# A selective scan that writes its states over its inputs: one pool of eight tiles in place of three and four

## The chip, the cores and the metric

The kernel runs on one core of a Trainium2 chip. The metric is the device time of one execution in microseconds (us). Before the change it is 21,997.85 us, the median of three runs (21,988.34 to 22,036.88).

The engines are named as the profile names them: PE multiplies matrices, PEld loads its weights, DVE is the vector engine, ACT the scalar engine, POOL is GpSimd, and SP issues the transfers. [...] SBUF and PSUM are the on-chip memories; PE writes to PSUM.

## The reference

Eight images of 56 x 56 tokens with 192 channels go through two layers. The first is an attention with depthwise convolutions. The second is a selective scan in four directions (by rows, by columns, and both backwards), and nearly all of the time is spent there. Cut to what matters:

```python
# xs: the 384 inner channels of each token, in the order of the direction k
dts, Bs, Cs = jnp.split(x_dbl, [R, R + N], axis=2)          # N = 16 states
delta = jax.nn.softplus(dts @ dt_w + dt_bias)               # per channel and token
A = -jnp.exp(A_logs)                                        # per channel and state

def step(h, inp):                                           # one token after another
    u_l, d_l, B_l, C_l = inp
    dA  = jnp.exp(d_l[..., None] * A)
    dBu = d_l[..., None] * B_l[:, :, None, :] * u_l[..., None]
    h = dA * h + dBu
    y = jnp.sum(h * C_l[:, :, None, :], axis=-1)            # sum over the 16 states
    return h, y
# ... then the four directions are added, normalised, gated with silu(z) and projected
```

## The kernel before

An image is cut into seven chunks of T = 448 tokens, so that there are 8 x 4 x 7 = 224 steps (image b, direction k, chunk c). In each step 16 states n are worked through, one after another. The 384 channels are NJ = 3 blocks of 128 partitions; a tile of [128, 3, 448] float32 is one state.

The pools (a pool hands out its buffers in turn; a tile can be written again when all of its readers are done):

```python
s2 = ctx.enter_context(tc.tile_pool(name="s2", bufs=2))
s3 = ctx.enter_context(tc.tile_pool(name="s3", bufs=3))     # dbu, g
s4 = ctx.enter_context(tc.tile_pool(name="s4", bufs=4))     # bb, h
py = ctx.enter_context(tc.tile_pool(name="py", bufs=1, space=PSUM))   # y
pa = ctx.enter_context(tc.tile_pool(name="pa", bufs=2, space=PSUM))   # da
pb = ctx.enter_context(tc.tile_pool(name="pb", bufs=3, space=PSUM))   # "bank": ht, cm, all else
```

One step:

```python
for n in range(NST + 1):
    if n < NST:
        bb = s4.tile([128, T], F32, name="bb")                        # B of this state on all partitions
        nc.sync.dma_start(bb, rows[n, :].partition_broadcast(128))
        ...                                                           # cm: C of this state, for six states
        dbu = s3.tile([128, NJ, T], F32, name="dbu")
        nc.gpsimd.tensor_tensor(                                      # L652, POOL
            dbu, du, bb.unsqueeze(1).to_broadcast([128, NJ, T]), ALU.mult)
        h = s4.tile([128, NJ, T], F32, name="h")
        for j in range(NJ):
            da = pa.tile([128, 512], F32, name="da")
            nc.scalar.activation(da[:, :T], dl[:, j], AF.Exp,         # L657, ACT
                                 scale=acoef[:, k * NJ + j, n:n + 1])
            nc.vector.tensor_tensor_scan(                             # L659, DVE
                h[:, j, rev], da[:, 0:T][:, rev], dbu[:, j, rev],
                0.0 if ci == 0 else carry[:, j, n:n + 1], ALU.mult, ALU.add)
        nc.scalar.copy(newc[:, :, n:n + 1], h[:, :, last])            # L662, ACT: the state carried on
        done.append((n, h, cm))
    if n >= 1:
        add_state(*done[n - 1], y, ct)
    ...            # a part of prepare() for the next step, of finish() for the image before,
    ...            # and of front(), the first layer of the next image
```

How a state gets into y, summed by PE in PSUM. States 0, 6 and 11 are multiplied by C on DVE (L598), states 3, 8 and 13 on POOL (L601), the other ten are transposed by PE, scaled by ACT and transposed back:

```python
def add_state(n, h, cm, y, ct):
    if n in BY_DVE:
        nc.vector.tensor_tensor(h, h, cm[:, :T]..., ALU.mult)         # L598
    elif n in BY_POOL:
        for j in range(NJ):
            nc.gpsimd.tensor_tensor(h[:, j], h[:, j], cm, ALU.mult)   # L601
    if n in BY_DVE or n in BY_POOL:
        for j in range(NJ):
            nc.tensor.matmul(y[:, j, :T], ident, h[:, j], ...)        # L604
        return
    for s in range(SUB):                                              # four quarters of 112 tokens
        ht = bank("ht")
        for j in range(NJ):
            nc.tensor.transpose(ht[...], h[:, j, cols], ident)        # L611
        g = s3.tile([TP, DIN], F32, name="g")
        nc.scalar.activation(g, ht[:TP, :DIN], AF.Copy, scale=ct[:, s, n:n + 1])   # L613
        for j in range(NJ):
            nc.tensor.matmul(y[:, j, cols], g[...], ident[:TP, :TP], is_transpose=True, ...)  # L615
```

What the next step needs, made by prepare() during this one (px, then xd, then softplus as below, then du):

```python
dl = s2.tile([128, NJ, T], F32, name="dl")
e = s1.tile([128, NJ, T], F32, name="e")
ln = s1.tile([128, NJ, T], F32, name="ln")
for j in range(NJ):
    ...                                                               # pdt (PE, L573)
    nc.scalar.activation(e[:, j], pdt[:, :T], AF.Abs, bias=dtb[:, q])   # L575
    nc.scalar.activation(dl[:, j], pdt[:, :T], AF.Relu, bias=dtb[:, q]) # L576
nc.scalar.activation(e, e, AF.Exp, scale=-1.0)                        # L578
nc.scalar.activation(ln, e, AF.Identity, bias=one)                    # L579
nc.vector.scalar_tensor_tensor(e, ln, -1.0, e, ALU.add, ALU.subtract) # L580
nc.scalar.activation(ln, ln, AF.Ln)                                   # L581
nc.vector.tensor_tensor(dl, dl, e, ALU.subtract)                      # L582
nc.vector.tensor_tensor(dl, dl, ln, ALU.add)                          # L583
du = s2.tile([128, NJ, T], F32, name="du")
nc.gpsimd.tensor_tensor(du, dl, xs, ALU.mult)                         # L585, POOL
```

A step ends with an addition of y to yacc on DVE (L690 for k = 0, L693 for the others). In the steps with k = 0 the image before is finished: means by PE, `yc` on DVE (L479), its square `sq` on POOL (L481), the variance by PE (L494), `yc` scaled on DVE (L498, L500), times the gate on POOL (L501), then the projection `pout` on PE (L510, L513), copied to `ot` by ACT (L516). In the other steps of images 0 to 6, and in all steps of image 0, a slice of front() for the next image is worked in.

The program is written in the order above, but the instructions of each engine are put into its queue by a scheduler, which takes into account how many buffers there are.

Of the kernel before, what the change touches and what calls it, by code (L numbers as in the profile page):

```python
# [8 lines left out]
F32 = mybir.dt.float32  # L9
AF = mybir.ActivationFunctionType  # L10
ALU = mybir.AluOpType
# [10 lines left out]
T = 448  # L22
# [12 lines left out]
NJ = DIN // 128  # L35
# [12 lines left out]
def kernel(  # L48
# [24 lines left out]
    nc = tc.nc  # L73
# [7 lines left out]
    def fill(name, shape, value):  # L81
        t = const.tile(shape, F32, name=name)
        nc.vector.memset(t, value)
        return t
# [5 lines left out]
    one = fill("one", [128, 1], 1.0)  # L90
# [81 lines left out]
    s1 = ctx.enter_context(tc.tile_pool(name="s1", bufs=1))  # L172
    s2 = ctx.enter_context(tc.tile_pool(name="s2", bufs=2))
    s3 = ctx.enter_context(tc.tile_pool(name="s3", bufs=3))
    s4 = ctx.enter_context(tc.tile_pool(name="s4", bufs=4))
    py = ctx.enter_context(tc.tile_pool(name="py", bufs=1, space=PSUM))
    pa = ctx.enter_context(tc.tile_pool(name="pa", bufs=2, space=PSUM))
    pb = ctx.enter_context(tc.tile_pool(name="pb", bufs=3, space=PSUM))
# [2 lines left out]
    def bank(name):  # L181
        return pb.tile([128, 512], F32, name=name, tag="bank")
# [337 lines left out]
    def finish_pools(b):  # L520
        es = ExitStack()
        c1 = es.enter_context(tc.tile_pool(name=f"c1_{b}", bufs=1))
        c2 = es.enter_context(tc.tile_pool(name=f"c2_{b}", bufs=2))
        return es, (c1, c2, scaled_weights(c1, 1, made[b]["rstd"]))
# [9 lines left out]
    def view(t, k, c):  # L534

        if k % 2 == 0:
            return t[:, :, c * T:(c + 1) * T].rearrange("p j (a b) -> p j a b", b=HW)
        return t.rearrange("p j (h w) -> p j w h", w=HW)[:, :, c * RPC:(c + 1) * RPC, :]
# [3 lines left out]
    def prepare(b, k, c, i):  # L542

        xs = s2.tile([128, NJ, T], F32, name="xs")
        nc.sync.dma_start(xs, made[b]["xcs"][k % 2][:, :, c * T:(c + 1) * T])
        if i == 0:
            dtw = s2.tile([R, DIN], F32, name="dtw")
            nc.sync.dma_start(dtw, dt_wT[:, k, :])
            dtws[k] = dtw
        yield {}  # L550
        px = bank("px")
        for j in range(NJ):
            nc.tensor.matmul(px[:NR, :T], xpw[:, k, j], xs[:, j], start=(j == 0), stop=(j == NJ - 1))
        xd = s2.tile([NR, T], F32, name="xd")
        nc.scalar.copy(xd, px[:NR, :T])
        rows = dchunk.tile([2 * NST, T], F32, name="rows")
        nc.sync.dma_start(rows, xd[R:NR, :])
        st = {"xs": xs, "xd": xd, "rows": rows}
        yield st

        pct = bank("pct")
        for s in range(SUB):
            nc.tensor.transpose(pct[:TP, s * NR:(s + 1) * NR], xd[:, s * TP:(s + 1) * TP], ident[:NR, :NR])
        ct = s2.tile([TP, SUB, NST], F32, name="ct")
        nc.scalar.copy(ct, pct[:TP, :SUB * NR].rearrange("p (s r) -> p s r", r=NR)[:, :, R + NST:NR])
        st["ct"] = ct

        dl = s2.tile([128, NJ, T], F32, name="dl")
        e = s1.tile([128, NJ, T], F32, name="e")
        ln = s1.tile([128, NJ, T], F32, name="ln")  # L570
        for j in range(NJ):
            pdt = bank("pdt")
            nc.tensor.matmul(pdt[:, :T], dtws[k][:, j * 128:(j + 1) * 128], xd[0:R, :], start=True, stop=True)  # L573
            q = k * NJ + j
            nc.scalar.activation(e[:, j], pdt[:, :T], AF.Abs, bias=dtb[:, q])  # L575
            nc.scalar.activation(dl[:, j], pdt[:, :T], AF.Relu, bias=dtb[:, q])  # L576
            yield st
        nc.scalar.activation(e, e, AF.Exp, scale=-1.0)  # L578
        nc.scalar.activation(ln, e, AF.Identity, bias=one)  # L579
        nc.vector.scalar_tensor_tensor(e, ln, -1.0, e, ALU.add, ALU.subtract)  # L580
        nc.scalar.activation(ln, ln, AF.Ln)  # L581
        nc.vector.tensor_tensor(dl, dl, e, ALU.subtract)  # L582
        nc.vector.tensor_tensor(dl, dl, ln, ALU.add)  # L583
        du = s2.tile([128, NJ, T], F32, name="du")
        nc.gpsimd.tensor_tensor(du, dl, xs, ALU.mult)  # L585
        st["dl"], st["du"] = dl, du
        yield st
# [30 lines left out]

    total = sum(front(0))
    cur = run_all(prepare(*steps[0]))  # L620
    carry = None
    fill, spent, given = None, 0.0, 0
    es = None
    for i, (b, k, c, ci) in enumerate(steps):
        if k == 0 and ci == 0:
            if b > 0:
                es, pools = finish_pools(b - 1)
            first_slot = 0 if b == 0 else NCH * NST
            fill = front(b + 1) if b + 1 < nb else iter(())
            spent, slot = 0.0, 0  # L630
        ending = finish(b - 1, c, pools) if k == 0 and b > 0 else iter(())
        ahead = prepare(*steps[i + 1]) if i + 1 < len(steps) else iter(())
        nxt = None
        rev = slice(None, None, -1 if k >= 2 else 1)
        last = slice(0, 1) if k >= 2 else slice(T - 1, T)
        dl, du, xd, rows, ct, xs = (cur[v] for v in ("dl", "du", "xd", "rows", "ct", "xs"))
        y = py.tile([128, NJ, 512], F32, name="y")
        newc = s2.tile([128, NJ, NST], F32, name="newc")
        done = []
        for n in range(NST + 1):  # L640
            if n < NST:
                bb = s4.tile([128, T], F32, name="bb")
                nc.sync.dma_start(bb, rows[n, :].partition_broadcast(128))
                cm = None
                if n in BY_DVE:
                    cm = bank("cm")
                    nc.tensor.matmul(cm[:, :T], sel[:, BY_DVE.index(n), :], xd, start=True, stop=True)  # L647
                elif n in BY_POOL:
                    cm = s2.tile([128, T], F32, name="cb")
                    nc.sync.dma_start(cm, rows[NST + n, :].partition_broadcast(128))  # L650
                dbu = s3.tile([128, NJ, T], F32, name="dbu")
                nc.gpsimd.tensor_tensor(  # L652
                    dbu, du, bb.unsqueeze(1).to_broadcast([128, NJ, T]), ALU.mult)
                h = s4.tile([128, NJ, T], F32, name="h")
                for j in range(NJ):
                    da = pa.tile([128, 512], F32, name="da")
                    nc.scalar.activation(da[:, :T], dl[:, j], AF.Exp,  # L657
                                         scale=acoef[:, k * NJ + j, n:n + 1])
                    nc.vector.tensor_tensor_scan(  # L659
                        h[:, j, rev], da[:, 0:T][:, rev], dbu[:, j, rev],  # L660
                        0.0 if ci == 0 else carry[:, j, n:n + 1], ALU.mult, ALU.add)
                nc.scalar.copy(newc[:, :, n:n + 1], h[:, :, last])  # L662
                done.append((n, h, cm))
            if n >= 1:
                add_state(*done[n - 1], y, ct)
            if n >= 2 and n % 2 == 0:
                nxt = next(ahead, nxt)
            if n < NST:
                for _ in range(2):
                    next(ending, None)  # L670
                slot += 1
                want = total * (slot - first_slot) / (NTOK - NST - first_slot)
                while spent < want:
                    got = next(fill, None)
                    if got is None:
                        break
                    spent += got
        for _ in ending:
            pass
        if k == 0 and ci == NCH - 1 and b > 0:  # L680
            es.close()
        if k == NDIR - 1 and ci == NCH - 2:
            for _ in fill:
                pass
        for st in ahead:
            nxt = st
        yv = view(yacc, k, c)
        if k == 0:
            for j in range(NJ):
                nc.vector.scalar_tensor_tensor(yacc[:, j, c * T:(c + 1) * T], xs[:, j], dsum[:, j], y[:, j, :T],  # L690
                                               ALU.mult, ALU.add)
        else:
            nc.vector.tensor_tensor(yv, y[:, :, :T].rearrange("p j (a b) -> p j a b", b=HW), yv, ALU.add)  # L693
        carry, cur = newc, nxt
# [63 lines left out]
```

## Time and profile before

The profiled execution took 21,992 us. Its core had a mean granted TensorE clock of 0.92 of full speed. From the groups of instructions:

| engine, line | what | count | mean ns | busy us |
|---|---|---|---|---|
| POOL L652 | dbu = du * B | 3584 | 3040 | 10,845.1 |
| POOL L601 | h * C, three states of 16 | 2016 | 1272 | 2,508.1 |
| DVE L659 | scan, with a carried state | 9216 | 1134 | 10,006.9 |
| DVE L659 | scan, first chunk | 1536 | 1072 | 1,579.6 |
| ACT L657 | da = exp(dl * A) | 10752 | 638 | 6,795.8 |
| ACT L613 | g = ht * C | 8960 | 576 | 4,786.1 |
| PE L611 | transposes into ht | 26880 | 288 | 4,483.0 |
| PE L615 | transposes back into y | 26880 | 281 | 4,360.3 |
| PE L604 | h into y by the identity | 8064 | 611 | 3,805.4 |

A line of the wait list reads: engine, tile and line that waited <- engine, tile and line that it waited for: us in total, how often, the longest. A line of the timeline reads: start, us taken, engine, line, operation, out<-in, shapes, and how many in a row; in brackets the idle time before, and what ended it. A wait for several things is put down to the one that came last.

### The profile page before, as it was taken

To read this page: it belongs to the slowest core of one execution; us is meant where nothing else is said; L and a number is where in the kernel's file an instruction comes from. 1 tells how busy PE (TensorE), PEld (TensorE's weight loads), DVE (VectorE), ACT (ScalarE), POOL (GpSimd) and SP (SyncE) were. 2 spreads that over 40 slices of the span, in tenths; PEclk is the share of its full clock that TensorE was granted. 3 is DMA by queue.
4 is the path that set the end of the run, shared out by engine and by line. 5 is a ranking of instruction groups with operands and counts; after the bars stand their busy time and mean duration, and the time that the engine had idled before them with its cause. 6 is when DMAs were issued, how large, how long until landed. Compare 5 with 4: busy or idle time off the path is not lost. (4 is left out here: it accounts for less than half of the span.)

```text
span 21990.5 us, 246125 instructions
## 1 busy us (share of the span) xinstructions
PE 18854.4 (86%) x84640; PEld 11005.3 (50%) x84640; DVE 15390.6 (70%) x14585; ACT 14548.1 (66%) x28166; POOL 14468.7 (66%) x6131
## 2 busy tenths in 40 slices
PE   8889888899888998889888899888988889887776
PEld 4454555545455455554555545555455554554444
DVE  1477777766677666876677766777667776677775
ACT  2467667666675766757666676666767667677665
POOL 0467677666676667766677666776667666677775
PEclk9899999999999999999999999999999999998888
DMA  1222222222222222222223222222222222222221
GB/s 50 82 66 66 67 84 65 74 62 65 82 68 71 63 69 77 81 61 61 73 75 80 60 62 73 76 77 62 61 84 68 76 61 61 81 70 67 61 61 41
DMA packets 935285, 1508.59 MB, mean 69 GB/s; under 512 B 102480, under 2 KB 917904, under 8 KB 930960
## 3 DMA queue, kind: packets, MB, share of 16 engines
q1 hardware_dynamic: 934032, 1492.83, 24.3%
q8 instruction: 670, 10.98, 0.2%
q14 instruction: 583, 4.78, 0.1%
HBM read 1322.38 MB, written 170.08 MB: 68 GB/s over the span
## 5 line engine op out<-in xcount | busy, mean ns | idle before, releaser
L652 POOL TENSOR_TENSOR dbu<-du,bb 128x1344 f32<-128x1344 f32 x3584 | 10845.1, 3040 | 4585.7 <-DVE h L659 2376.8
L659 DVE TENSOR_TENSOR_SCAN h<-da,newc,dbu 128x448 f32<-128x448 f32 x9216 | 10006.9, 1134 | 4142.2 <-PE ht L611 1467.0
L657 ACT ACTIVATE da<-dl,acoef 128x448 f32<-128x448 f32 x10752 | 6795.8, 638 | 3454.9 <-DVE h L659 3423.1
L613 ACT ACTIVATE g<-ht,ct 112x384 f32<-112x384 f32 x8960 | 4786.1, 576 | 1364.1 <-PE ht L611 1331.2
L615 PE MATMUL y<-ident,g 112*128 112x112 f32 x26880 | 4360.3, 281 | 1316.2 <-ACT g L613 1276.1
L611 PE MATMUL ht<-ident,h 128*112 128x128 f32 x26880 | 4483.0, 288 | 671.5 <-DVE h L659 182.1
L615 PEld LDWEIGHTS y<-ident,g 112*128 112x128 f32 x26880 | 2994.2, 147 | 3629.3 <-ACT g L613 3017.1
L604 PE MATMUL y<-h,ident 128*128 128x448 f32 x8064 | 3805.4, 611 | 473.2 <-DVE h L598 207.5
L611 PEld LDWEIGHTS ht<-ident,h 128*112 128x112 f32 x26880 | 3213.5, 141 | 1978.7 <-issue 1012.7
L601 POOL TENSOR_TENSOR h<-h,cb 128x448 f32<-128x448 f32 x2016 | 2508.1, 1272 | 1374.7 <-ACT newc L662 1374.7
L604 PEld LDWEIGHTS y<-h,ident 128*128 128x128 f32 x8064 | 1588.3, 211 | 2092.7 <-issue 1472.4
L659 DVE TENSOR_TENSOR_SCAN h<-da,dbu 128x448 f32<-128x448 f32 x1536 | 1579.6, 1072 | 676.2 <-PE ht L611 209.2
L662 ACT COPY newc<-h 128x3 f32<-128x3 f32 x3584 | 702.9, 196 | 1267.6 <-DVE h L659 1260.8
L215 PE MATMUL pcv<-xa,dg 128*128 128x440 f32 (+2 forms) x3024 | 1303.0, 545 | 0.3 <-ACT g L613 0.3
L388 PE MATMUL ps<-qT,kT 64*112 64x448 f32 x2352 | 1160.3, 605 | 70.3 <-DMA qT<-qd 38.3
L598 DVE TENSOR_TENSOR h<-h,cm 128x1344 f32<-128x1344 f32 x672 | 1035.9, 1542 | 255.8 <-PE cm L647 244.2
L396 PE MATMUL po<-pT,vt 112*128 112x448 f32 x2352 | 1043.1, 550 | 0.0
L585 POOL TENSOR_TENSOR du<-dl,xs 128x1344 f32<-128x1344 f32 x224 | 679.8, 3035 | 540.6 <-DVE dl L583 526.2
L391 ACT ACTIVATE pT<-ps,nsh 112x448 f32<-112x448 f32 x1176 | 726.1, 630 | 290.9 <-PE ps L388 237.8
L215 PE MATMUL pq<-band,dgq 96*96 96x440 f32 (+3 forms) x2016 | 866.4, 546 | 0.0
L647 PE MATMUL cm<-xd,sel 44*128 44x448 f32 x1344 | 712.0, 611 | 6.5 <-ACT dl L576 6.5
L573 PE MATMUL pdt<-xd,dtw 12*128 12x448 f32 x1344 | 708.0, 607 | 0.0
(140 smaller groups left out, 12929.0 us busy)
## 6 DMA issues: line engine op xcount, KB each, us to landing
bb<-rows SPq DMA_DIRECT2D x3584, 224.0 KB
cb<-rows SPq DMA_DIRECT2D x672, 224.0 KB
xt<-x1d SPq DMA_DIRECT2D x224, 336.0 KB
xs<-xch SPq DMA_DIRECT2D x112, 672.0 KB
xs<-xcw SPq DMA_DIRECT2D x112, 672.0 KB
xch<-xv SPq DMA_DIRECT2D x24, 1568.0 KB
xcw<-xw SPq DMA_DIRECT2D x168, 224.0 KB
xin<-in_x_dram SPq DMA_DIRECT2D x56, 336.0 KB
```

The lines of the kernel that those rows point to most:

```text
L215: nc.tensor.matmul(out[:, o0:o1, a:b], lhs, img(lo, hi)[:, :, a + dx - 1:b + dx - 1], start=(t == TAPS[0]), stop=(t == TAPS[-1]))
L388: nc.tensor.matmul(ps[:TP, :T], kh[rows, kb * TP:(kb + 1) * TP], qh[rows, :], start=True, stop=True)
L396: nc.tensor.matmul(po[:, :T], vt[:, kb, g:g + 2, :].rearrange("p g d -> p (g d)"), pts[kb], start=(kb == 0), stop=(kb == NKB - 1))
L598: nc.vector.tensor_tensor(h, h, cm[:, :T].unsqueeze(1).to_broadcast([128, NJ, T]), ALU.mult)
L601: nc.gpsimd.tensor_tensor(h[:, j], h[:, j], cm, ALU.mult)
L604: nc.tensor.matmul(y[:, j, :T], ident, h[:, j], start=(n == 0), stop=(n == NST - 1))
L611: nc.tensor.transpose(ht[:TP, j * 128:(j + 1) * 128], h[:, j, cols], ident)
L613: nc.scalar.activation(g, ht[:TP, :DIN], AF.Copy, scale=ct[:, s, n:n + 1])
L615: nc.tensor.matmul(y[:, j, cols], g[:, j * 128:(j + 1) * 128], ident[:TP, :TP], is_transpose=True, start=False, stop=(n == NST - 1 and s = ...
L652: nc.gpsimd.tensor_tensor(dbu, du, bb.unsqueeze(1).to_broadcast([128, NJ, T]), ALU.mult)
L657: nc.scalar.activation(da[:, :T], dl[:, j], AF.Exp, scale=acoef[:, k * NJ + j, n:n + 1])
L659: nc.vector.tensor_tensor_scan(h[:, j, rev], da[:, 0:T][:, rev], dbu[:, j, rev], 0.0 if ci == 0 else carry[:, j, n:n + 1], ALU.mult, ALU.add)
```

## The change

The scan writes each state over the product that it reads. A state then needs one tile from its product to its last reader, where it needed one tile in s3 from the product to the scan, and one in s4 from the scan to its last reader. The seven tiles become one pool of eight. The room for the eighth comes from `ln`, whose values are now kept in `du` until du itself is written. The change is for a freer use of the same memory: which part of the chain runs ahead is no longer fixed at three and four.

```diff
@@ -173,6 +173,7 @@
     s4 = ctx.enter_context(tc.tile_pool(name="s4", bufs=4))
+    s8 = ctx.enter_context(tc.tile_pool(name="s8", bufs=8))
@@ -567,7 +568,7 @@
-        ln = s1.tile([128, NJ, T], F32, name="ln")
+        du = s2.tile([128, NJ, T], F32, name="du")
...
-        nc.scalar.activation(ln, e, AF.Identity, bias=one)
-        nc.vector.scalar_tensor_tensor(e, ln, -1.0, e, ALU.add, ALU.subtract)
-        nc.scalar.activation(ln, ln, AF.Ln)
+        nc.scalar.activation(du, e, AF.Identity, bias=one)
+        nc.vector.scalar_tensor_tensor(e, du, -1.0, e, ALU.add, ALU.subtract)
+        nc.scalar.activation(du, du, AF.Ln)
         nc.vector.tensor_tensor(dl, dl, e, ALU.subtract)
-        nc.vector.tensor_tensor(dl, dl, ln, ALU.add)
-        du = s2.tile([128, NJ, T], F32, name="du")
+        nc.vector.tensor_tensor(dl, dl, du, ALU.add)
         nc.gpsimd.tensor_tensor(du, dl, xs, ALU.mult)
@@ -648,16 +648,15 @@
-                dbu = s3.tile([128, NJ, T], F32, name="dbu")
+                h = s8.tile([128, NJ, T], F32, name="h")
                 nc.gpsimd.tensor_tensor(
-                    dbu, du, bb.unsqueeze(1).to_broadcast([128, NJ, T]), ALU.mult)
-                h = s4.tile([128, NJ, T], F32, name="h")
+                    h, du, bb.unsqueeze(1).to_broadcast([128, NJ, T]), ALU.mult)
                 for j in range(NJ):
...
                     nc.vector.tensor_tensor_scan(
-                        h[:, j, rev], da[:, 0:T][:, rev], dbu[:, j, rev],
+                        h[:, j, rev], da[:, 0:T][:, rev], h[:, j, rev],
                         0.0 if ci == 0 else carry[:, j, n:n + 1], ALU.mult, ALU.add)
```

## The prediction

> **What bounds the kernel now.** I read the head of the page first, then the wait list, then the timeline of one step (448 tokens, one direction, 16 states) in each kind of stage.
>
> ```profile
> span 21990.5 us, 246125 instructions
> ...
> PE 18854.4 (86%) x84640; PEld 11005.3 (50%) x84640; DVE 15390.6 (70%) x14585; ACT 14548.1 (66%) x28166; POOL 14468.7 (66%) x6131
> ```
>
> No engine is full. [...] the rest stand at about two thirds. The time is made of engines waiting for each other, so next come the waits:
>
> ```profile
> ACT da L657 <- DVE h L659: 3423.1, 4200, 7.1
> PEld y L615 <- ACT g L613: 3017.1, 4588, 7.3
> POOL dbu L652 <- DVE h L659: 2376.8, 1006, 13.3
> DVE h L659 <- PE ht L611: 1676.1, 750, 8.9
> ...
> POOL h L601 <- ACT newc L662: 1374.7, 196, 17.7
> ...
> DVE h L659 <- PE y L604: 833.0, 391, 8.4
> ```
>
> Two are waits for buffers. The scan on DVE waits for PE to be done with the state four back (1676.1 + 833.0 = 2509 us, 11% of the span), and POOL's product waits for the scan three back (2376.8 us, on an engine with time to spare). Now the stages. The period of a step is the distance of two additions to yacc in the timeline. A step that carries a slice of the next image's first layer (I call it a fill step):
>
> ```profile
> 4963.67 1.55 DVE L693 TENSOR_TENSOR yacc<-y,yacc 128x1344 f32<-128x1344 f32 x1
> ...
> 5031.08 6.11 POOL L601 TENSOR_TENSOR h<-h,cb 128x448 f32<-128x448 f32 x3 [10.62 <-ACT newc L662]
> 5037.15 3.03 POOL L585 TENSOR_TENSOR du<-dl,xs 128x1344 f32<-128x1344 f32 x1
> ...
> 5058.22 1.53 DVE L693 TENSOR_TENSOR yacc<-y,yacc 128x1344 f32<-128x1344 f32 x1
> ```
>
> Here 94.6 us. A step of the last image, with no fill (one call of these: a bare step):
>
> ```profile
> 21048.36 1.53 DVE L693 TENSOR_TENSOR yacc<-y,yacc 128x1344 f32<-128x1344 f32 x1
> ...
> 21107.88 3.04 POOL L652 TENSOR_TENSOR dbu<-du,bb 128x1344 f32<-128x1344 f32 x1 [2.17 <-issue]
> 21107.94 4.40 DVE L580 SCALAR_TENSOR_TENSOR e<-ln,e 128x1344 f32<-128x1344 f32 x1 [0.18 <-ACT ln L579]
> ...
> 21117.43 3.02 POOL L585 TENSOR_TENSOR du<-dl,xs 128x1344 f32<-128x1344 f32 x1 [6.51 <-DVE dl L583]
> ...
> 21133.70 1.53 DVE L693 TENSOR_TENSOR yacc<-y,yacc 128x1344 f32<-128x1344 f32 x1
> ```
>
> 85.3 us, and du starts when the softplus chain (L580, L582, L583) ends. A step that also finishes the image before (k = 0):
>
> ```profile
> 19783.65 2.42 POOL L481 TENSOR_TENSOR sq<-yc 128x1344 f32<-128x1344 f32 x1
> ...
> 19806.17 3.02 POOL L501 TENSOR_TENSOR yc<-yc,zs 128x1344 f32<-128x1344 f32 x1 [1.76 <-DVE yc L500]
> ...
> 19809.24 2.15 PE L510 MATMUL pout<-outpw,yc 128*112 128x192 f32 x6 [2.27 <-POOL yc L501]
> ```
>
> Its period is 85.2 us (first yacc addition at 19774.08, then 19859.33); PE waits for POOL's yc. From the yacc additions over the span: 28 fill steps of the first image at 91.8 us, 126 later ones at 99.5, 49 finishing ones at 85.7, 21 bare ones at 84.1. With 757 us of start and 189 of end that is 22,019, near enough to the span.
>
> [...] L580 takes 1.53 us as a rule and 4.40 where it began 0.06 us after a dbu of 3.04. [...] I expect the same duration in place.
>
> **The change part by part.** (1) No instruction is added or removed: 3584 products, 10752 scans, the same matmuls. Using du for ln costs nothing (two buffers, and the old du is dead). (2) DVE no longer waits for a free h: the product's tile is the scan's. The wait moves to POOL, which now needs the state eight back to be through PE. (3) The order of each queue moves, as the compiled programs show. I write the states 0 to 15 for POOL's products, C3, C8, C13 for its multiplications by C, and name a step's queue on POOL:
> - bare: before du C13 0-6 C3 7-11 C8 12-15; after du C13 0-9 C3 10-14 C8 15. ACT, DVE and PE keep their order.
> - finishing: before du 0-4 sq 5 6 C3 7 yc 8-11 C8 12-15 C13; after du 0-7 sq 8 9 C3 10-12 yc 13 C8 14 15 C13.
> - fill: before du 0-6 C3 7-11 C8 12-15 C13; after mostly du 0-6 C3 7-10 C8 11-13 C13 14 15. Softplus on DVE moves from between scans 13 and 15 to behind scan 15. On ACT, g of a state stood on average 2.5 states behind da (at most 3.7), now 4.1 (at most 7.7).
>
> Bare steps, from the start of du: C3 began at 34.6 us. Ten products in a row behind C13 end at 6.3 + 10 x 3.04 = 36.7, so C3 is 2.1 later. C8 began at 57.95; product 14 needs state 6 through PE, now at about 55.3, so C8 begins at 58.3, +0.35. The last product is then long done when L580 comes, and L580 falls from 4.40 to 1.53 us on the chain that sets du: -2.87. Sum -2.5 us x 21 = -53 us.
>
> Finishing steps: yc waited only for DVE and began at 41.4 us after du. In the new queue C3 ends at 39.3 and three products stand ahead of yc: 39.3 + 3 x 3.04 = 48.4, 7 later. PE's queue has pout ahead of the next cm and transposes, ACT's has ot ahead of g of state 5, and ACT is all but full from there to du; I let 1.5 to 2 us be recovered: +5.3 us x 49 = +260 us.
>
> Fill steps: the slot waits on DVE go (seven of them, 13.9 us, in the step shown). What comes: scan 14 waits for scan 13, C13 (3.3) and product 14 (3.0), some 6.7 us; at the end of a step DVE waits for g of states 9 and 10 on ACT (about 9), the softplus on two engines (about 5.5), du and product 0 (6.1): some 17 us beyond the 67 us that DVE is busy in such a step. So the scan chain alone takes 67 + 6.7 + 17 = 91 us. PE needs some 84 of the 99.5. Two chains of 91 and 84 us coupled through eight buffers, with g queued far behind da, I put at 97, an estimate with 4 us of doubt: -2.5 x 126 = -315 us. The first image's steps, with less PE work, I leave as they are.
>
> Sum: -53 + 260 - 315 = -108 us, 21,890. As I have counted every new wait but not what the looser coupling does for the others, I take 21,850.
>
> **The rivals.** (a) The buffers were the bound: all of the 2509 us come back, up to 19,500. Against it: in the fill steps PE is idle only a tenth of the time, and bare steps have hardly any slot wait. Half of it would be 20,700. (b) The new POOL wait closes a longer loop: PE frees a tile, POOL writes it (3.0), DVE scans it (3.4), and only then comes the g that PE waits for, since ACT takes it after da of seven states on. Some 9 us for one state where 99.5 / 16 = 6.2 are needed. Where the queue stands at its deepest lag in most steps, fill steps go to 102 and the time to 22,450. (c) POOL was never the limit and PE's queue is the same, so nothing moves: 21,990.
>
> **Range and chances.** The fill steps carry the doubt: 4 us either way is 500 us. The finishing steps add 150. Range 21,200 to 22,500. Faster than 21,558 needs fill steps of about 94 or less: 0.27. Slower than 22,438 needs them at 101 with the finishing loss: 0.19. The rest 0.54.
>
> **What would show it.** "DVE h <- PE" nearly gone from the wait list, and "POOL h <- PE" grown. L580 at 1.5 us and a bare step at 82.9. A finishing step at 90 to 91, with PE's pout waiting some 9 us for yc. In fill steps a gap on DVE of some 6 us ahead of scan 14 and one of 15 us or more ahead of scan 0. I am wrong if fill steps fall below 93 (coupling was the cost) or the scan's own duration moves.

## The result and the profile after

The changed kernel takes 23,683.09 us (median of four runs, 23,672.54 to 23,687.91), the kernel before 22,007.75 beside it: a ratio of 1.0759, 95% interval 1.0741 to 1.0778. The prediction was 21,850 us, range 21,200 to 22,500.

The head of the page of the changed kernel:

```profile
span 23685.2 us, 249153 instructions
...
PE 19449.3 (82%) x84640; PEld 11326.1 (48%) x84640; DVE 15504.3 (65%) x14585; ACT 14590.6 (62%) x28166; POOL 14256.4 (60%) x6131
```

The same work is done: DVE, ACT and POOL are busy for about as long as before, PE for 595 us more, in a span that is 1,695 us longer. The scan in place has its old duration, as the prediction expected, and so has the product (1,134 and 3,040 ns before; the mean in ns is the number after the busy time, in the groups of instructions):

```profile
L652 POOL TENSOR_TENSOR h<-du,bb 128x1344 f32<-128x1344 f32 x3584 | 10810.0, 3038 | 3369.3 <-PE ht L611 2086.4
L658 DVE TENSOR_TENSOR_SCAN h<-da,newc,h 128x448 f32<-128x448 f32 x9216 | 9963.2, 1133 | 4361.8 <-POOL h L652 2821.0
```

So the time went into waits. From the wait list of the changed kernel (us in total, times, longest):

```profile
...
ACT da L656 <- DVE h L658: 3670.2, 3702, 11.4
DVE h L658 <- POOL h L652: 3306.1, 806, 11.7
POOL du L585 <- DVE dl L584: 2930.0, 143, 26.5
POOL h L652 <- PE ht L611: 2086.4, 605, 11.9
...
POOL h L601 <- ACT newc L661: 1644.6, 369, 16.6
...
DVE h L598 <- PE cm L647: 1266.9, 200, 14.6
...
POOL h L652 <- PE y L604: 737.6, 234, 15.8
```

The 2,509 us in which the scan waited for PE are gone, as they had to be. In their place the scan waits 3,306 us for POOL's product, and the product waits 2,824 us for PE (2,086.4 + 737.6). In the kernel before, the scan's wait for the product was 452 us:

```profile
DVE h L659 <- POOL dbu L652: 452.2, 201, 4.5
```

Where the time was lost is read from the yacc additions. The period of a step is the time from the start of the addition before it to the start of its own, counted the same way for both kernels; the very first step has no addition before it.

| steps | before, us | after, us | number | together, us |
|---|---|---|---|---|
| first image | 90.7 | 95.4 | 27 | +126 |
| finishing | 85.8 | 92.4 | 49 | +319 |
| fill | 99.2 | 109.5 | 126 | +1,290 |
| bare | 84.1 | 81.7 | 21 | -50 |

The last column is worked out from periods that are not rounded. Its sum is +1,685, the time ahead of the first addition and behind the last adds 9, and the spans differ by 1,695. Three quarters of the loss lies in the fill steps. Here is how one of them looks inside, in the timeline of the changed kernel:

```profile
5346.83 0.82 PE L611 MATMUL ht<-ident,h 128*112 128x128 f32 x6
...
5350.28 3.03 POOL L652 TENSOR_TENSOR h<-du,bb 128x1344 f32<-128x1344 f32 x1 [2.98 <-PE ht L611]
...
5353.34 2.19 DVE L658 TENSOR_TENSOR_SCAN h<-da,newc,h 128x448 f32<-128x448 f32 x2 [2.65 <-POOL h L652]
5354.52 0.64 ACT L656 ACTIVATE da<-dl,acoef 128x448 f32<-128x448 f32 x1 [2.68 <-DVE h L658]
5355.10 0.56 ACT L613 ACTIVATE g<-ht,ct 112x384 f32<-112x384 f32 x1
...
5355.71 0.68 PE L615 MATMUL y<-ident,g 112*128 112x112 f32 x3 [1.76 <-ACT g L613]
...
5358.88 1.04 PE L611 MATMUL ht<-ident,h 128*112 128x128 f32 x6
...
5360.00 3.03 POOL L652 TENSOR_TENSOR h<-du,bb 128x1344 f32<-128x1344 f32 x1 [6.70 <-PE ht L611]
...
5363.07 1.15 DVE L658 TENSOR_TENSOR_SCAN h<-da,newc,h 128x448 f32<-128x448 f32 x1 [5.03 <-POOL h L652]
```

Read the brackets downwards. The product waits for PE to transpose an old state out of its tile; the scan waits for the product; the decay factor on ACT waits for the scan (it needs the PSUM tile that the scan has read); the weighted copy g of an old state, which stands behind that decay factor in ACT's queue, comes next; PE's transposition back waits for g, and only then does PE transpose what frees the next tile. From one product to the next it is 5360.00 - 5350.28 = 9.7 us, where the product itself takes 3.03. This is the longest distance in the step. Over all fill steps a wait for PE ended ahead of 633 of the 1,890 products that follow another in their step, and these start a median of 7.7 us behind the one before. All four engines take turns. And at the end of the same step, on DVE:

```profile
5382.03 0.60 DVE L411 BATCH_NORM_STATS2 st<-x 96x6 f32<-96x448 f32 x1
5393.17 1.55 DVE L598 TENSOR_TENSOR h<-h,cm 128x1344 f32<-128x1344 f32 x1 [10.55 <-PE cm L647]
5395.05 1.56 DVE L581 SCALAR_TENSOR_TENSOR e<-du,e 128x1344 f32<-128x1344 f32 x1 [0.32 <-ACT du L580]
...
5398.59 1.56 DVE L584 TENSOR_TENSOR dl<-dl,du 128x1344 f32<-128x1344 f32 x1 [0.39 <-ACT du L582]
5406.39 2.19 DVE L658 TENSOR_TENSOR_SCAN h<-da,newc,h 128x448 f32<-128x448 f32 x2 [6.24 <-POOL h L652]
```

For 24 us DVE scans nothing, and it is idle for 17.5 of them (the brackets). Two things could be behind this picture, and they call for different cures: a ring of tiles (a pool's buffers, used in turn) that is used up, or a preparation of the next step that comes too late.

### The profile page after: what moved, and what is told of

It is laid out like the page before. It is cut to its first block, busy times and chain, and to the rows that moved or that the text cites. A ratio compares the mean times of both kernels' runs of the same rounds, so it can differ in the third digit from the quotient of the medians.

```text
span 23685.2 us, 249153 instructions
## 1 busy us (share of the span) xinstructions
PE 19449.3 (82%) x84640; PEld 11326.1 (48%) x84640; DVE 15504.3 (65%) x14585; ACT 14590.6 (62%) x28166; POOL 14256.4 (60%) x6131
## 5 line engine op out<-in xcount | busy, mean ns | idle before, releaser
L652 POOL TENSOR_TENSOR h<-du,bb 128x1344 f32<-128x1344 f32 x3584 | 10810.0, 3038 | 3369.3 <-PE ht L611 2086.4
L658 DVE TENSOR_TENSOR_SCAN h<-da,newc,h 128x448 f32<-128x448 f32 x9216 | 9963.2, 1133 | 4361.8 <-POOL h L652 2821.0
L615 PE MATMUL y<-ident,g 112*128 112x112 f32 x26880 | 4477.2, 288 | 1983.1 <-ACT g L613 1951.3
L615 PEld LDWEIGHTS y<-ident,g 112*128 112x128 f32 x26880 | 3086.8, 151 | 4339.8 <-ACT g L613 3709.0
L604 PE MATMUL y<-h,ident 128*128 128x448 f32 x8064 | 3986.9, 634 | 519.9 <-POOL h L601 276.4
L601 POOL TENSOR_TENSOR h<-h,cb 128x448 f32<-128x448 f32 x2016 | 2336.4, 1186 | 1648.2 <-ACT newc L661 1644.6
L604 PEld LDWEIGHTS y<-h,ident 128*128 128x128 f32 x8064 | 1665.8, 222 | 2317.3 <-issue 1547.2
L658 DVE TENSOR_TENSOR_SCAN h<-da,h 128x448 f32<-128x448 f32 x1536 | 1596.6, 1083 | 739.3 <-POOL h L652 485.1
L574 PE MATMUL pdt<-xd,dtw 12*128 12x448 f32 x1344 | 773.2, 658 | 32.1 <-DVE hkv L304 32.0
L216 PEld LDWEIGHTS pcv<-xa,dg 128*128 128x128 f32 x3024 | 551.9, 204 | 353.2 <-issue 335.8
```

The lines of the kernel that those rows point to most:

```text
L216: nc.tensor.matmul(out[:, o0:o1, a:b], lhs, img(lo, hi)[:, :, a + dx - 1:b + dx - 1], start=(t == TAPS[0]), stop=(t == TAPS[-1]))
L604: nc.tensor.matmul(y[:, j, :T], ident, h[:, j], start=(n == 0), stop=(n == NST - 1))
L615: nc.tensor.matmul(y[:, j, cols], g[:, j * 128:(j + 1) * 128], ident[:TP, :TP], is_transpose=True, start=False, stop=(n == NST - 1 and s = ...
L652: nc.gpsimd.tensor_tensor(h, du, bb.unsqueeze(1).to_broadcast([128, NJ, T]), ALU.mult)
L658: nc.vector.tensor_tensor_scan(h[:, j, rev], da[:, 0:T][:, rev], h[:, j, rev], 0.0 if ci == 0 else carry[:, j, n:n + 1], ALU.mult, ALU.add)
```

## The experiments

I call the lead the number of states by which ACT's queue has the decay factors da ahead of the weighted copy g. It is read from the compiled queues. ACT works through its queue in that order, for its records in the traces give the same leads: at most 3.67 before and 7.67 after (four and eight tiles less a third of a state). It grew only in the steps with fill: in the finishing steps it is at most 3.33 before and 3.67 after, in the bare ones 2 in both. C3, C8 and C13 are POOL's multiplications, as in the prediction; VectorE and GpSimd in the expectations are DVE and POOL. All ratios are to the kernel before, run beside each on the same chip (21,990 to 22,008 us). The last four columns are periods of a step in us.

| run | us | ratio, 95% interval | first image | finishing | fill | bare |
|---|---|---|---|---|---|---|
| before | 22,007.75 | 1 | 90.7 | 85.8 | 99.2 | 84.1 |
| after | 23,683 | 1.0759 (1.0741 to 1.0778) | 95.4 | 92.4 | 109.5 | 81.7 |
| e1_three_five | 22,224 | 1.0111 (1.0073 to 1.0148) | 91.9 | 85.2 | 101.0 | 84.1 |
| e5_two_six | 22,698 | 1.0326 (1.0289 to 1.0364) | 91.8 | 95.4 | 100.2 | 87.8 |
| e2_pool_6 | 24,901 | 1.1329 (1.1287 to 1.1370) | 104.8 | 90.5 | 118.8 | 76.2 |
| e6_cap4 | 21,771 | 0.9905 (0.9868 to 0.9942) | 88.8 | 92.4 | 95.8 | 81.7 |
| e7_pin | 23,289 | 1.0592 (1.0571 to 1.0613) | 95.4 | 85.4 | 109.1 | 81.7 |
| e8_cap_pin | 21,446 | 0.9757 (0.9741 to 0.9774) | 89.0 | 85.8 | 95.6 | 81.7 |
| e9_cap_pool6 | 21,505 | 0.9781 (0.9762 to 0.9801) | 87.5 | 90.2 | 95.5 | 76.4 |
| e10_cap6 | 21,984 | 1.0001 (0.9992 to 1.0010) | 90.4 | 92.4 | 97.0 | 81.7 |
| e11_c_late | 23,213 | 1.0550 (1.0525 to 1.0575) | 93.2 | 89.7 | 107.5 | 80.2 |
| e12_cap_c_early | 23,159 | 1.0525 (1.0499 to 1.0551) | 94.0 | 103.9 | 99.8 | 88.9 |
| e13_best | 21,230 | 0.9647 (0.9629 to 0.9665) | 87.5 | 85.3 | 95.5 | 76.1 |
| e3_early | 24,742 | 1.1244 (1.1211 to 1.1276) | 103.9 | 94.6 | 115.2 | 81.2 |

### Is it the lead or the sharing? Eight tiles that are not shared

e1_three_five is the kernel before with ln in du and five tiles for h; e5_two_six has two tiles for dbu and six for h.

```diff
...
-                h = s4.tile([128, NJ, T], F32, name="h")
+                h = s4.tile([128, NJ, T], F32, name="h", bufs=5)     # e5: dbu bufs=2, h bufs=6
```

> Eight tiles as in the changed kernel, but not shared: three for the scan's inputs and five for its states, and the scan writes to a tile of its own. ACT's queue puts the decay factors at most 4.67 states ahead of the weighted copy g (3.67 in the kernel before, 7.67 in the changed one), 3.2 on average (2.5 and 4.1). Theory D (the loss comes from how far the scans are queued ahead of what TensorE has to do with the states, so that the next step's preparation comes late): in proportion to the average, (3.16 - 2.52) / (4.1 - 2.52) = 0.4 of the loss, near 22,690 us. Theory S (the loss comes from the sharing, since a product must wait until TensorE has read the state in its tile): nothing is shared here, so no loss and 21,950 to 22,050 us. Rival P (VectorE and GpSimd disturb each other on one tile): as S.

> Two tiles for inputs and six for states, not shared. The decay factors run up to 5.67 states ahead, 3.67 on average. Theory D: (3.67 - 2.52) / 1.58 = 0.73 of the loss, near 23,240 us, and the wait of GpSimd's delta product for VectorE grows from 526 us of the kernel before to over 1,500 us. Theory S: no loss through states; two input tiles can cost a little on GpSimd, 22,000 to 22,300 us, and the wait for the delta product stays near 526 us.

Measured: 22,224 and 22,698 us. Neither theory has the numbers. The lead rose to 5.67 in e5_two_six, and the fill steps went up by only 1.0 us (99.2 to 100.2): a long lead by itself costs little, so D falls as a theory of the fill steps. Most of e5's loss is in the finishing steps (49 x 9.6 = 470 us), which D and S don't speak of; I did not take that apart.

### Fewer shared tiles

e2_pool_6 is the changed kernel with `bufs=6` for s8.

> The changed kernel with six shared tiles in place of eight. The decay factors run up to 5.67 states ahead, 3.5 on average. Theory D: 0.64 of the loss, near 23,090 us, faster than the changed kernel though it has fewer tiles. Theory S: a product waits for TensorE two states earlier, so at least as slow as the changed kernel, 23,700 to 24,500 us.

Measured: 24,901 us, fill steps 118.8, the scans' wait for products 6,020 us. D is refuted again, and S was too mild. The same lead of 5.67 costs 1 us in a fill step with tiles that are not shared, and some 20 with six that are (C8 and C13 also stand early there, which is worth a few of them, as shown below, and there are six tiles in all in place of eight).

### The lead held short, tiles and sharing kept

e6_cap4 gives ACT an order, and no wait: the third da of a state stands behind the last g of the state four earlier.

```diff
...
+                    gate = last_g[-4 if n == 0 else -3] if j == NJ - 1 and len(last_g) > 3 else None
+                    with tc.issue_after(gate) if gate is not None else ExitStack():
-                    nc.scalar.activation(da[:, :T], dl[:, j], AF.Exp,
-                                         scale=acoef[:, k * NJ + j, n:n + 1])
+                        nc.scalar.activation(da[:, :T], dl[:, j], AF.Exp,
+                                             scale=acoef[:, k * NJ + j, n:n + 1])
```

`last_g` holds the last g of each state, or that of the state before where a state has none.

> The changed kernel, eight shared tiles, with an order and no wait added on ACT: the third decay factor of a state is queued behind the last weighted copy of the state four earlier, so that the lead is at most 3.67 states as in the kernel before (2.7 on average), while the tiles and their sharing stay. Theory D: the loss goes, 21,950 to 22,300 us, the delta product's wait for VectorE falls from 2,930 us to near 526 us, and a fill step is back near 99 us. Theory S, and rival P (both engines on one tile): the tiles are shared as before, so 23,500 to 23,800 us.

Measured: 21,771 us, 1,912 less than the changed kernel and 1% below the kernel before. Theory D had 21,950 at the least. From its wait list, whole span:

```profile
...
POOL h L601 <- ACT newc L666: 2777.3, 261, 21.1
...
POOL du L585 <- DVE dl L584: 778.0, 95, 18.3
POOL h L655 <- PE y L604: 774.4, 327, 15.7
POOL h L655 <- PE ht L611: 666.0, 379, 17.1
...
DVE h L663 <- POOL h L655: 441.6, 188, 4.1
```

The scans' wait for products is 442 us in place of 3,306. The step that was shown above, in this kernel (POOL, and one line of DVE; the product is L655 here):

```profile
5068.99 6.16 POOL L601 TENSOR_TENSOR h<-h,cb 128x448 f32<-128x448 f32 x3 [17.07 <-ACT newc L666]
5075.11 3.03 POOL L585 TENSOR_TENSOR du<-dl,xs 128x1344 f32<-128x1344 f32 x1
5078.22 20.95 POOL L655 TENSOR_TENSOR h<-du,bb 128x1344 f32<-128x1344 f32 x7
5081.29 8.44 DVE L663 TENSOR_TENSOR_SCAN h<-da,newc,h 128x448 f32<-128x448 f32 x8 [4.06 <-POOL h L655]
```

POOL idles too, 17 us, but ahead of C13 with all 16 products of the step delivered. It makes du while DVE is at the last scans, and then seven products in a row. DVE waits 4.06 us for the first of them and scans from 5081.29 on: between the last scan of a step and the first of the next it is 4 us here and 24 in the changed kernel. The scheduler, given this bound, also puts C8 and C13 behind products 12 and 15 again in most fill steps, which is taken apart below. Sharing and the second engine on one tile are in this kernel as they were, so S and P fall as sole causes. What is left is their meeting: shared tiles and a lead that takes all of them. I call this theory R; what should count is tiles less lead, 0.33 in the changed kernel, 4.33 here.

### Tiles less lead

e9_cap_pool6 is e6_cap4 with six tiles, e10_cap6 is e6_cap4 with the bound at six states earlier (`last_g[-6 if n == 0 else -5]`).

> Six shared tiles, the lead capped at 3.67 states (six tiles with their own lead of 5.67 took 24,901 us, eight with 3.67 took 21,771). Theory R (the loss needs both: tiles that are shared and a lead in ACT's queue that uses all of them, so that a product on GpSimd waits for TensorE at once; what counts is tiles less lead, here 2.3): most of the loss goes, 21,800 to 22,200 us. Theory D (lead alone): as the capped kernel with eight tiles, 21,770 us. Theory T (number of shared tiles alone): near 24,900 us.

> Eight shared tiles, the lead capped at 5.67 states, 3.8 on average. Theory R: tiles less lead is 2.3 as with six tiles and 3.67, so about the same time as that kernel, 21,800 to 22,200 us. Theory D (lead alone): between the capped kernel (2.7 on average, 21,771 us) and the changed one (4.1, 23,683 us), near 23,270 us. Theory T: number of tiles alone, 23,683 us. Rival C (not the lead: in the changed kernel GpSimd's multiplication of state 13 stands ahead of the products of 14 and 15, here it stands behind them as in the kernel before): 21,770 to 21,900 us.

Measured: 21,505 and 21,984 us; their fill steps take 95.5 and 97.0. Six shared tiles are as good as eight there once the lead is 3.67, and a lead of 5.67 is good with eight tiles (97.0) and bad with six (118.8). That is R. The range for e9 was too high: with six tiles in place of eight the bare steps also go from 81.7 to 76.4, the finishing ones from 92.4 to 90.2 and those of the first image from 88.8 to 87.5, some 250 us together, which no theory had. In the bare steps C3 stands behind product 7 there, behind 9 with eight tiles, in queues that are otherwise close; that this is the reason was not tried. e10 equals the kernel before in total, 6.6 us worse in finishing steps and 2.2 better in fill steps; it is above rival C's range, but e10 alone could not exclude C.

### The place of POOL's multiplications

In most fill steps of the changed kernel C8 and C13 stand early: C8 ahead of product 10 or 11, C13 ahead of products 14 and 15. e11_c_late puts them back and leaves the lead alone; e12_cap_c_early puts them early in the capped kernel, though not quite where the changed one has them: C3 stands one or two products earlier, C13 one later. ADD_AT names the states that are added at each n, and muls holds POOL's multiplications.

```diff
 # e11_c_late: C3, C8 and C13 are issued behind products 6, 11 and 15
-            if n >= 1:
-                add_state(*done[n - 1], y, ct)
+            for m in ADD_AT.get(n, ()):
+                with tc.issue_after(prod.ins) if m in BY_POOL else ExitStack():
+                    add_state(*done[m], y, ct)
...
 # e12_cap_c_early: products 5, 10 and 15 are issued behind C3, C8 and C13
+                gate_c = muls.get(n - 2)
+                with tc.issue_after(gate_c) if gate_c is not None else ExitStack():
-                nc.gpsimd.tensor_tensor(
-                    h, du, bb.unsqueeze(1).to_broadcast([128, NJ, T]), ALU.mult)
+                    nc.gpsimd.tensor_tensor(
+                        h, du, bb.unsqueeze(1).to_broadcast([128, NJ, T]), ALU.mult)
```

> The changed kernel with nothing altered but the place of GpSimd's multiplications in its queue: C3, C8 and C13 stand behind the products of states 6, 11 and 15, as in the kernel before (in the changed one C8 stands ahead of product 10 and C13 ahead of products 14 and 15). The lead of the decay factors over the weighted copies stays, 7.67 at most and 5.4 on average in the fill steps. Theory C (the place of these multiplications closes a loop: the next products stand behind a multiplication that waits for scan 8 or 13): the fill steps fall from 109.5 to 97 or less, near 22,100 us. Theory R (shared tiles and a lead that uses all of them): still 23,500 to 23,700 us. Halfway would say that both count.

> The converse: the capped kernel (lead 3.67, eight shared tiles, 21,771 us) with GpSimd's multiplications put early, C3, C8 and C13 ahead of products 5, 10 and 15. Theory C: the loss comes back in part or whole, 22,500 to 23,400 us. Theory R: 21,750 to 21,950 us, since the lead leaves four tiles free.

Measured: 23,213 and 23,159 us. In the totals both seem to count, and the stages tell them apart. In fill steps the late place gains 2.0 us (109.5 to 107.5) with the long lead, and the early place costs 4.0 (95.8 to 99.8) with the short one; the lead makes 107.5 - 95.8 = 11.7 with C late, and 109.5 - 99.8 = 9.7 with C early. So R carries the fill steps, and C is a small part. e11_c_late and e10_cap6 show it best: eight shared tiles and C late in both, a lead of 7.67 and of 5.67, fill steps of 107.5 and 97.0. About half of e12's loss is elsewhere: +11.5 in finishing steps (565 us) and +7.2 in bare ones (150 us). From its wait list:

```profile
POOL h L601 <- ACT newc L669: 6706.9, 646, 32.6
...
DVE h L666 <- POOL h L658: 1495.9, 495, 6.6
```

A multiplication with only one more product ahead of it than its own state's makes POOL wait for the scan of that state (6,707 us, 2,777 in e6_cap4), and the products behind it come late too. I read this as the same fault by another way, POOL losing its distance to DVE; it was not taken further.

### Is it the late preparation?

The other reading of DVE's gap at the end of the step. e3_early lets prepare() go on at every state.

```diff
-            if n >= 2 and n % 2 == 0:
+            if n >= 1:
                 nxt = next(ahead, nxt)
```

> The changed kernel with the next step's preparation advanced at every state in place of every second one: on ACT the decay rate's Abs and Relu stand at state 10.9 of a fill step (14.2 in the changed kernel, 13.5 in the run with eight tiles and a lead of 5.67), VectorE's last softplus addition at 12.4 (14.9 in both), so that GpSimd has the delta product and the first products of the next step before the last scans. The lead stays at 7.67 at most and grows to 7.2 on average in fill steps. Theory L (the loss is the late preparation: softplus, delta product, product 0 and scan 0 one after another at the end of each step): the fill steps fall to 97 or less, 22,000 to 22,300 us, the wait of the scans for products from 3,306 us to under 1,000. Theory R (a lead that uses all shared tiles): no gain, 23,400 to 24,500 us, that wait stays at 3,000 us or more.

Measured: 24,742 us, fill steps 115.2: theory L has the wrong sign. The waits within 21 fill steps of the third image, first of the changed kernel, then of e3_early:

```profile
DVE h L658 <- POOL h L652: 479.6, 113, 10.3
ACT da L656 <- DVE h L658: 439.7, 363, 8.6
...
POOL du L585 <- DVE dl L584: 364.5, 17, 25.9
POOL h L652 <- PE ht L611: 299.2, 76, 10.5
```

```profile
DVE h L658 <- POOL h L652: 794.3, 242, 9.4
POOL h L652 <- PE ht L611: 697.8, 161, 11.5
ACT da L656 <- DVE h L658: 637.3, 437, 9.5
...
POOL h L652 <- PE y L604: 262.4, 74, 13.1
```

The wait for du is all but gone (43.0 us in these 21 steps, 364.5 in the changed kernel), as intended. What POOL then waits for is PE and its tiles: 697.8 + 262.4 = 960 us, 46 per step. e3_early alone does not settle it, since its lead is also longer on average, as expected above. e10_cap6 does: the last addition of the softplus stands as late in its queue as in the changed kernel (state 14.9 in both), and du still waits 259 us for it in the same 21 steps:

```profile
POOL du L585 <- DVE dl L584: 259.4, 17, 17.8
...
DVE h L663 <- POOL h L655: 122.0, 21, 6.3
```

Yet its fill steps take 97.0 us. So the late preparation was how the used-up ring showed at the end of a step, not why it was slow. The wait of the scans for products, in the same 21 steps of each kernel and divided by 21, follows the lead: 1.6 us before, 2.2 in e6_cap4, 5.8 in e10_cap6, 20.0 in e11_c_late, 22.8 in the changed kernel, 37.8 in e3_early.

### The finishing steps

They take the same 92.4 us with the lead held (e6_cap4), so their loss is another one. e7_pin and e8_cap_pin hold POOL's order there.

```diff
...
+        pins["sq"] = nc.gpsimd.tensor_tensor(sq, yc, yc, ALU.mult).ins
...
+        pins["yc"] = nc.gpsimd.tensor_tensor(yc, yc, zs, ALU.mult).ins
...
+                gate_p = pins.get("yc" if n >= 8 else "sq" if n >= 5 else "")
+                with tc.issue_after(gate_p) if gate_p is not None else ExitStack():
                     nc.gpsimd.tensor_tensor(h, du, bb..., ALU.mult)
```

> The changed kernel with GpSimd's order in the finishing steps put back near that of the kernel before: the products of states 5 on are queued behind the square, and those of 8 on behind the product with the gate (yc), which the changed kernel has behind products 11 or 12. Theory F (the finishing steps lost through this order, TensorE waiting for yc): finishing steps from 92.4 back to 85 to 87 us, 49 x -6.5 = -320, near 23,370 us, the fill steps stay at 109.5. Rival (they lose through the shared tiles or through ACT's order, as the fill steps do): they stay at 92 and the time at 23,600 to 23,750 us.

> Both orders held: the lead of the decay factors over the weighted copies at most 3.67 states, and GpSimd's order in the finishing steps as in the kernel before. With theory F the gain of the finishing steps adds to the 21,771 us of the capped kernel: 21,771 - 320 = 21,450 us, ratio near 0.975. With its rival 21,750 to 21,800 us.

Measured: 23,289 and 21,446 us. The finishing steps are back at 85.4 and 85.8, and nothing else moved by more than 0.4 us. Theory F holds, and the two losses add. Both edits hold the square as well as yc, so which of the two counts more is not shown.

### A version that beats both

e13_best is e8_cap_pin with six shared tiles.

> Six shared tiles, the lead capped at 3.67 and the square and yc held in the finishing steps. From the run with six tiles and the cap (finishing steps 90.2, bare steps 76.4, 21,505 us): finishing steps from 90.2 to the 85 to 87 us of the kernel before give -49 x 4 = -200, 21,300 us. If what holds the finishing steps at 90 with six tiles is something other than yc, 21,450 to 21,520 us.

Measured: 21,230 us, ratio 0.9647 (0.9629 to 0.9665). Head of its page:

```profile
span 21241.4 us, 249431 instructions
...
PE 18533.6 (87%) x84640; PEld 10913.1 (51%) x84640; DVE 15223.7 (72%) x14585; ACT 14500.1 (68%) x28166; POOL 14370.5 (68%) x6131
```

Six tiles where the kernel before used seven, and 3.5% faster: the scan in place is a good change, with its queues held. Whether the old pools would gain from orders like these was not tried.

## Why the prediction was wrong

- **The failed step: "Two chains of 91 and 84 us coupled through eight buffers, with g queued far behind da, I put at 97".** Measured 109.5. The 84 for PE was an estimate of mine; in the 21 fill steps of the third image, before the change, PE was busy 87.2 us a step (1,831 in all). The coupling was given 6 us over the chain of 91, and it took 18.5 over that chain as it stands. With the lead held the fill step is 95.8 (e6_cap4), 4.8 over it. Of the other 13.7, 11.7 go with the lead, which closes the loop, and 2.0 with the place of POOL's multiplications. In the same 21 steps of the changed kernel the scans waited 22.8 us a step for products, where the prediction's sum has 12.8 (6.7 for scan 14, 6.1 for du and product 0). Rival (b) had the right loop ("some 9 us for one state": a median of 7.7 where PE released the product, 9.7 in the step shown) and too small a step (102). I treated "where the queue stands at its deepest lag in most steps" as unlikely, and gave the fill steps an average lag of 4.1 states. That is the average over all steps: in the fill steps alone it is 5.4 (3.1 before), counted in the ACT records of the two traces at the first g of each state.
- **The idle time of 17 us at the end of a fill step: right in size**, 17.5 us in the one step shown. But e3_early takes the preparation off that chain and the time grows. A sum of pieces along a chain says little where the ring decides when each piece may begin.
- **The first image's steps, "I leave as they are"**: 90.7 to 95.4, +126 us. They carry fill too and share the fault: 88.8 with the lead held, 89.0 with POOL's order also held.
- **The finishing steps, +5.3 us: right in the order that costs the time, small in size.** The step got 6.5 longer. In the changed kernel's timeline PE's pout waits for yc:

```profile
21354.30 3.02 POOL L502 TENSOR_TENSOR yc<-yc,zs 128x1344 f32<-128x1344 f32 x1
21357.37 0.77 PEld L511 LDWEIGHTS pout<-outpw,yc 128*112 128x112 f32 x3 [5.21 <-POOL yc L502]
```

  Over the 49 steps yc begins at a median of 48.7 us after du, where the prediction had 48.4 (41.4 before). But PE waits 5.2 us for it (2.5 before) and not 9, and hardly any of the 7 us was won back, where the prediction let ACT and PE recover "1.5 to 2 us". The square is late too, 27.1 us after du in place of 18.9, and the prediction did not count it. Why a wait of PE that is 2.7 us longer comes with a step that is 6.5 us longer is not shown; that POOL's order makes the loss is (e7_pin).
- **The bare steps, -2.5 us: right.** They got 2.4 shorter. The softplus instruction that the prediction followed (L580, now L581), in the 21 steps of before and of after (ns, shortest, median and longest):

```profile
L580 DVE SCALAR_TENSOR_TENSOR e<-ln,e x21: 1559/4390/4400, 20017.6 to 21701.8; 128x1344 f32<-128x1344 f32 x21
L581 DVE SCALAR_TENSOR_TENSOR e<-du,e x21: 1557/1559/1560, 21760.4 to 23398.5; 128x1344 f32<-128x1344 f32 x21
```

  In 20 of the 21 steps of before, one of POOL's products (3.03 to 3.04 us) began 0.05 to 0.11 us ahead of L580, which took 4.33 to 4.40 us. In the other one, and in all 21 of after, no instruction of POOL overlapped with it, and it took 1.56 us. That this alone shortens the step was not tried.
- **What buffers are for.** The prediction read the scan's 2,509 us of waiting for PE as waits for buffers. They went, as that reading says. But a tile too few was not what made the step long: six shared tiles in a held order (21,230 us in e13_best) are faster than seven or eight in the scheduler's (22,008 and 23,683).
- **Slips in the numbers.** The fill steps of the kernel before take 99.2 us and not 99.5, which accounts for the 28 us by which the prediction's sum of 22,019 is above the span. In rival (b), 102 us for a fill step gives 22,520 with the prediction's other terms, not 22,450; 22,438 needs 101.4, not 101. None of these changes the outcome.
- **Near the number by another kernel.** With the lead held, e6_cap4 takes 21,771 us and its fill steps 95.8, near the 21,850 and the 97 predicted. This does not show that the sum was right: the prediction was made for the queues with a lead of 7.67, and e6_cap4 has others. It does show that the change of buffers alone need not cost anything; the order of the queues that came with it did.

What stays open: why e5_two_six loses in its finishing and bare steps, why six tiles shorten the bare steps, whether the square or yc makes the loss of the finishing steps, and how much of the fill steps' loss comes through the lower clock (below).

## What to carry to other kernels

Where a scheduler fills the engines' queues, a buffer count is also an order: here each tile more let it queue the head of the chain one state further ahead of its tail (leads of 3.67 to 7.67 for four to eight tiles). Where the tiles were shared by the whole chain and the lead used them all, each engine waited for the one that frees the next tile. Count the lead in the queues, by kind of step, and keep it below the number of shared tiles: 0.33 left cost some 12 us of a fill step here, 2.33 left cost about 1 us or nothing, and what lies between was not tried. Hold the lead with an order rather than with a buffer. In the same way, put work that waits for a late result (C13) behind what other engines need from the same engine, and work that another engine waits for (yc) ahead of what can wait.

## What was not expected of the hardware

The mean granted TensorE clock was lower in the slower of these kernels: 0.929 in e13_best, 0.920 in the kernel before, 0.889 in the changed one, 0.864 in e3_early, 0.853 in e2_pool_6. For the same 84,640 matmuls PE's busy time rose from 18,534 to 20,335 us from the first to the last of these. In the 21 fill steps of the third image the clock was 0.93 in the kernel before, 0.93 in e6_cap4 and 0.88 in the changed kernel, and PE was busy 1,831, 1,799 and 1,920 us: from e6_cap4 to the changed kernel 5.7 us more a step, of 13.4 by which the step is longer. As an estimate, this is the most that the lower clock can have added there directly. Whether the waiting lowers the clock was not tested.

The scan in place costs next to nothing: in the changed kernel it takes 1,133 ns, against 1,134 with separate tiles in the kernel before, where a state is carried in, and 1,083 against 1,072 in the first chunk.
